# Three moves in the gated stage of a graph transformer: GpSimd's long third parts behind weight sums, and parts of the output weights behind gates and eviction sums

## The chip, the cores and the metric

The kernel runs on one core of a Trainium2 chip. The metric is the device time of one execution in microseconds (us). The core has a matrix engine (TensorE, PE in the profile), three engines for elementwise work (VectorE is DVE, ScalarE is ACT, GpSimd is POOL), and SyncE (SP), which here only issues transfers between the device's memory and the on-chip memory SBUF. Matmul results go to eight banks of another on-chip memory, PSUM. Each engine takes its own instructions strictly in order.

## The reference

A graph network with four transformer layers between two graph convolutions, on 1024 nodes with 512 features in float32. The change lies in the second half of each layer, the gated feed-forward part:

```python
for i in range(L):                                   # L = 4
    a = _attn(_ln(h, ln2_w[i], ln2_b[i]), cond, Wq[i], Wk[i], Wv[i], Wo[i])
    h = h + a
    u = _ln(h, ln3_w[i], ln3_b[i]) @ geglu_w[i] + geglu_b[i]   # 512 -> 4096
    val, gate = jnp.split(u, 2, axis=-1)
    f = val * jax.nn.gelu(gate, approximate=False)             # 2048 wide
    h = h + f @ ffo_w[i] + ffo_b[i]                            # 2048 -> 512
```

## The kernel before

**The gated stage.** For each layer, the product with `geglu_w` is cut into 4 x 4 pieces (r = 0 to 3, c = 0 to 3); each yields 128 columns of values and of gates on both halves of the nodes. The four pieces of r = 0 (class `Quad`) run first. The twelve of r = 1 to 3 are `Chunk` objects, named by layer, r and c; this text names one of layer 0 by r_c, so 3_3 is the last. A chunk is a fast scheme with seven products (numbers 0 to 6) in place of eight, and each float32 operand is split into three parts of a faster matmul form: a high part (`h`), a low part (`l`) and their difference (`s`, the third part). Each product is three pairs of matmuls: with h (first pair), with l (second), and, after ScalarE or VectorE has scaled the sum in its PSUM bank by 1 + TINY, with s. That makes 42 matmuls per chunk, 21 pairs. On the side of the nodes the parts (`gr`, `gl`) are there from the start. On the side of the weights each chunk's have to be made:

- SP loads the chunk's weights, `gxa` and `gxb` (`Chunk.__init__`, four transfers, called by `load()`).
- GpSimd forms the scheme's **sums** of the weights (`Chunk.sums`, L1097): three into `gxa`, one into `gy`, 128 x 256 each.
- ScalarE makes the high parts (L1060): `gha` (128 x 1024, the "long" one), `ghb` (128 x 512) and a 128 x 256 piece of `gs` from `gy` (the "short" ones).
- VectorE makes the low parts (L1061): `gla`, `glb`, and a piece of `gs`.
- GpSimd makes the third parts (L1066): `gsa` in two halves of 128 x 512, `gsb`, and a piece of `gs`.

A chunk uses gha, gla, gsa for products 0, 5, 6 and 4, ghb, glb, gsb for 1 and 3, gs for 2. All this is done ahead: while PE works at chunk m, the engines make the long parts of chunk m+1 and the sums of chunk m+2.

**Around the products.** `Chunk.steps` is a generator that the loop at the end of the listing drives step by step; the steps of chunk m-1 (`before` in the loop) are interleaved with those of chunk m (`flow`). ScalarE scales banks (L1139), copies product 0 (L1168) and applies the two gates, Gelu with a bias (L1152). VectorE adds products to running sums (L1160), does the scalings that take a term along, the **eviction sums** (L1143), and multiplies values by gates into the tile fT (L1191, L1193). SP stores fT to `f_dram` (L1209).

**The output stage** follows (class `Output`): eight units for each half of the nodes, each with a load `fr` of 256 columns of f and, in the first half, a load `wff` of 256 rows of `ffo_w`. Both are split in three: `ah_f` on ScalarE, `al_f`, `as_f` on VectorE for f (`Output.split`, L315 to L318); `bh_wff` on ScalarE, `bl_wff`, `bs_wff` on VectorE (two halves each) for the weights (`split_w`, L1244 to L1251). A unit is four blocks of six matmuls (L1270): bh with ah, bl with al, bs with as. Unit 0's weights are prepared during the gated stage: `ahead` yields after each of the five operations, one per chunk. f's first load is `output.fetch(0)`, its split `output.split(0)`; `fetch_w(u)` loads weights.

**What sets the order.** Instructions wrapped in `pin` stay in the order in which the program emits them, on their engine; the rest is placed by the scheduler at the times of its own model. So the order of the calls in the loop is by and large the order on each engine. `waiting_for(ins, engine)` makes all of GpSimd's instructions emitted in the block wait for `ins`: for the third parts that is `split_left.low`, the last low part made so far. The tiles come from a ring of 35 slots of 128 x 1024.

Of the kernel before, what the change touches and what calls it, by code (L numbers as in the profile page):

```python
# [26 lines left out]
def gnn_kernel(  # L27
# [37 lines left out]
    KC = D // P  # L65
# [4 lines left out]
    R = DFF // D  # L70
# [14 lines left out]
    @contextmanager  # L85
    def waiting_for(ins, engine):

        traced = nc.cur_bb.bb.instructions
        n = len(traced)
        yield  # L90
        for i in traced[n:]:
            if i.engine == engine:
                tc.add_manual_dep(i, ins.ins.name, mybir.DependencyInfo(
                    mybir.DependencyClass.Sync, mybir.DependencyReason.DATA))
# [454 lines left out]
    def project_steps(nb, hT, w, name, emit):  # L549

        ph = bank(f"hw_{name}_{nb}")
        c0 = (nb % 4) * P
        for k in range(KC):
            nc.tensor.matmul(ph, hT[nb // 4][k // 2][:, k % 2, c0:c0 + P],
                             w[k // 2][:, k % 2, :], start=(k == 0), stop=(k == KC - 1),
                             skip_group_check=True)
            yield
        emit(nb, ph)
# [132 lines left out]
    def add_left(left, rows, to, root, name):  # L691

        for d in range(NB):
            nc.sync.dma_start(left.rearrange("p a b -> p (a b)"), left_dram[d])
            pl = bank(f"left_{name}_{d}")
            for s in range(NB):
# [7 lines left out]
    steps = (step for nb in range(NB)  # L704
             for step in project_steps(nb, h0T, w_in, "in",
                                       lambda nb, ph: nc.scalar.copy(hs_in[nb], ph)))
# [11 lines left out]
    with ExitStack() as behind:  # L718
        for begun_by in (scaled_last, shifted_last):
            behind.enter_context(tc.issue_after(begun_by.ins))  # L720
        for t in range(ET):
            if t % (ET // (NB * KC)) == 0:
                next(steps)
            count(t)
        for _ in steps:
            pass
        first_v = bank("begun_v0")
        plain(first_v, raw_x[0, 0], 0, raw_wv, range(2))
        with tc.issue_after(load_dve.ins):
            for j in counted:  # L730
                if j % 2:
                    degrees(j // 2, C[j // 2], t512(f"part_{j // 2}"))
        with tc.issue_after(degrees.last.ins):
            plain(first_v, raw_x[0, 0], 0, raw_wv, range(2, KC))
        nc.scalar.copy(begun["v0"][0][:, 0, :], first_v)
# [66 lines left out]
    def acc_tile(name):  # L802
        return accs.tile([P, 512], F32, tag="acc", name=name)
# [271 lines left out]
    class Chunk:  # L1075
# [75 lines left out]
            cg = self.cv + DFF // P  # L1151
            pin(nc.scalar.activation(to, of, AF.Gelu, bias=gcols[:, cg:cg + 1]))  # L1152

        def steps(self, sum_next):


            n, bias = self.n, gcols[:, self.cv:self.cv + 1]

            def add(to, x, y):
                pin(nc.vector.tensor_tensor(to, x, y, OP.add))  # L1160

            self.banks = {}
            self.scale(0)
            yield
            self.scale(5)
            yield
            s1, u2, u3 = (acc_tile(f"g{x}_{n}") for x in ("s1", "u2", "u3"))
            pin(nc.scalar.copy(s1, self.end(0)))  # L1168
            self.scale(6)
            yield  # L1170
            add(u2, self.end(5), s1)
            yield
            sum_next()
            self.scale(4)
            add(u3, self.end(6), u2)
            self.scale_onto(1, s1)
            g1 = acc_tile(f"g1_{n}")
            d = self.end(4)
            add(g1, d, u3)
            add(u2, d, u2)  # L1180
            self.scale_onto(3, u3)
            self.scale_onto(2, u2)
            yield
            a = self.end(1)
            yield
            g0 = acc_tile(f"g0_{n}")
            self.gate(g0, self.end(3))
            self.gate(g1, g1)
            d = self.end(2)
            f0, f1 = self.f.of(self.c)  # L1190
            pin(nc.vector.scalar_tensor_tensor(f0, a, bias, g0, OP.add, OP.mult))  # L1191
            yield
            pin(nc.vector.scalar_tensor_tensor(f1, d, bias, g1, OP.add, OP.mult))  # L1193
            self.f.store(self.c)
# [263 lines left out]
    for l in range(L):  # L1458
# [261 lines left out]
        def load():  # L1720
            if chunks:
                ready.append(Chunk(l, *chunks.pop(0)))

        def sum_chunk(n):
            if n < len(ready):
                ready[n].sums()

        def begin_split(n, low, t=nc.gpsimd):
            flow = ready[n].split_steps(low, t) if n < len(ready) else iter(())
            next(flow, None)  # L1730
            return flow
# [7 lines left out]
        for c, q in enumerate(quads):  # L1739
            if c == 2:  # L1740
                long, short = (begin_split(0, low, nc.vector) for low in (False, True))
# [7 lines left out]
                load()  # L1749
        with waiting_for(split_left.last, mybir.EngineType.Pool):  # L1750
            sum_chunk(1)

        def split_rest(short):
            long = begin_split(0, False)
            next(long, None)
            with waiting_for(split_left.low, mybir.EngineType.Pool):
                for flow in short, long:
                    for _ in flow:
                        pass

        output = Output(l)
        ahead = output.ahead()
        before, short = None, iter(())
        for r in range(1, R):
            f = Gated(l, r)
            for c in range(KC):
                n = (r - R + 2) * KC + c
                if n == -1:
                    output.fetch_w(0)
                if (r, c) == (R - 1, KC - 2):  # L1770
                    output.fetch(0)
                chunk = ready.pop(0)
                flow = chunk.steps(lambda: sum_chunk(1))
                chunk.f = f
                next(flow)
                if 0 < n < 5:
                    next(ahead)
                for _ in islice(short, 2):
                    pass
                next(flow)  # L1780
                if before:
                    split_rest(short)
                    load()
                for _ in parts:
                    pass
                if (r, c) == (R - 1, KC - 1):
                    output.split(0)
                    output.fetch(1)
                for step in range(3):
                    if before:  # L1790
                        next(before, None)
                    next(flow)
                    if step == 0 and n == 0:
                        next(ahead)
                    if step == 1 and not before:
                        split_rest(iter(()))
                        load()
                before = flow
                short = begin_split(0, True)
        output.fetch_w(1)  # L1800
        output.fetch_w(2)
        for _ in range(3):
# [201 lines left out]
```

## Time and profile before

| what | value |
|---|---|
| median of 3 runs | 2320.28 us (2319.72 to 2321.01) |
| profiled execution's own time | 2319.71 us |
| its span, first to last instruction | 2317.9 us |
| granted TensorE clock, mean | 1.000 |
| gated chunks of layer 0 in the span | 445.49 to 565.76 us |
| PE busy in that window | 118.06 of 120.27 us |
| VectorE, ScalarE, GpSimd busy there | 108.47, 68.87, 89.52 us |

The profile is of one execution. A row of its timeline gives the start in us from the span's start, the duration, the engine, the line, the operation, and the tiles written and read, without their numbers; "x2" marks two merged instructions, and brackets say how long the engine was idle ahead of it and which instruction ended that. A row of the waits gives the total in us, the count and the longest. Matmul rows overlap: each is in the pipeline for longer than the interval to the next start, so starts are compared. One layer stands for all four: the stage begins at 445.49, 980.35, 1515.18 and 2049.99 us and takes 120.3 us each time.

### The profile page before, as it was taken

The page shows a single profiled execution, that of the slowest core. Times are in us where ns is not written, and L with a number is a line of the kernel's source. Part 1 is how long each engine was busy: PE and PEld are TensorE (multiplying, and loading weights), DVE is VectorE, ACT ScalarE, POOL GpSimd, SP SyncE. Part 2 cuts the span into 40 slices and gives each one's busy share as a digit, 9 for nine tenths or more (in the row PEclk, how much of TensorE's full clock was granted, in tenths as well). Part 3 has the DMA queues.
Part 4 walks back from the last instruction along what each step waited for, and adds up shares of the span by engine and source line. Part 5 has one row for each costly group of instructions (what it writes and reads, how often), then busy time and mean ns, then how long its engine had stood idle before and what let it go on. Part 6 is the DMA issues. An engine that isn't in the chain of part 4 may idle for free. (4 is left out here: it accounts for less than half of the span.)

```text
span 2317.9 us, 34192 instructions
## 1 busy us (share of the span) xinstructions
PE 2290.8 (99%) x12368; PEld 1730.7 (75%) x12368; DVE 1718.3 (74%) x3176; ACT 1101.5 (48%) x2159; POOL 799.7 (34%) x739
## 2 busy tenths in 40 slices
PE   8999999999999999999999999999999999999999
PEld 5668887577877887477886888577786888667777
DVE  9876556899975556989985555989986554889964
ACT  7544554565344445455344444556334444555410
POOL 1133223285032235177022334168022224158211
PEclk9999999999999999999999999999999999999999
DMA  6052120245411101134521111133532111033551
GB/s 204 2 160 87 55 96 6 69 119 177 151 64 65 54 24 37 56 117 128 182 82 69 53 40 37 35 107 106 182 135 69 36 43 51 10 109 119 182 191 37
DMA packets 161072, 205.46 MB, mean 89 GB/s; under 512 B 11304, under 2 KB 101744, under 8 KB 160896
## 3 DMA queue, kind: packets, MB, share of 16 engines
q1 hardware_dynamic: 158800, 197.77, 25.9%
q0 software_dynamic: 1376, 4.30, 0.6%
q8 instruction: 102, 1.67, 0.3%
q10 hardware_dynamic: 720, 1.11, 0.1%
q14 instruction: 74, 0.61, 0.1%
HBM read 152.80 MB, written 50.34 MB: 88 GB/s over the span
## 5 line engine op out<-in xcount | busy, mean ns | idle before, releaser
L321 POOL TENSOR_TENSOR as_c<-ah_c,al_c 128x512 fp32r<-128x512 f32 x128 | 191.5, 1526 | 405.1 <-DVE al_c L316 338.4
L1139 ACT ACTIVATE g<-g 128x512 f32<-128x512 f32 x192 | 112.5, 586 | 145.3 <-PE g L1125 145.3
L378 ACT ACTIVATE k<-k 128x512 f32<-128x512 f32 x125 | 72.2, 584 | 227.4 <-PE k L367 227.4
L1270 PE MATMUL fx<-bs_wff,as_f 128*128 128x512 f32 x512 | 158.9, 390 | 0.6 <-DVE as_f L318 0.6
L1270 PE MATMUL fy<-bl_wff,al_f 128*128 128x512 f32 x512 | 158.9, 390 | 0.6 <-DVE al_f L316 0.5
L1270 PE MATMUL fy<-bh_wff,ah_f 128*128 128x512 f32 x512 | 157.7, 389 | 0.2 <-ACT ah_f L315 0.2
L848 ACT ACTIVATE pr<-sc,nmax 128x256 f32<-128x256 f32 x256 | 118.4, 475 | 76.2 <-DVE nmax L843 75.5
L315 ACT ACTIVATE ah_f<-fr 128x1024 fp32r<-128x1024 f32 x64 | 67.9, 1060 | 176.2 <-PE fy L1270 101.0
L383 DVE COPY kT<-k 128x512 f32<-128x512 f32 x54 | 37.2, 688 | 143.9 <-PE k L367 143.9
L367 PE MATMUL v<-bh_wv,ah_c 128*128 128x512 f32 x508 | 142.8, 403 | 0.0
L367 PE MATMUL v<-bs_wv,as_c 128*128 128x512 f32 x508 | 142.2, 402 | 0.1
L367 PE MATMUL k<-ah_c,bh_wk 128*128 128x512 f32 x500 | 136.9, 395 | 0.0
L367 PE MATMUL v<-bl_wv,al_c 128*128 128x512 f32 x508 | 136.2, 390 | 0.0
L367 PE MATMUL k<-al_c,bl_wk 128*128 128x512 f32 x500 | 134.0, 390 | 0.0
L367 PE MATMUL k<-as_c,bs_wk 128*128 128x512 f32 x500 | 132.3, 395 | 0.2
L378 ACT ACTIVATE v<-v 128x512 f32<-128x512 f32 x127 | 75.0, 590 | 115.7 <-PE v L367 115.7
L853 DVE TENSOR_SCALAR pr<-pr,inv 128x256 f32<-128x256 f32 x256 | 127.3, 540 | 2.3
L1125 PE MATMUL g<-gr,gsa 128*128 128x512 f32 x384 | 122.8, 401 | 4.8 <-ACT g L1139 4.8
L1125 PE MATMUL g<-gr,gha 128*128 128x512 f32 x384 | 120.0, 394 | 0.0
L1125 PE MATMUL g<-gl,gla 128*128 128x512 f32 x384 | 118.4, 389 | 0.0
L1066 POOL TENSOR_TENSOR gsa<-gha,gla 128x512 fp32r<-128x512 f32 x88 | 112.4, 1300 | 16.9 <-DVE gla L1061 16.9
L920 POOL TENSOR_TENSOR os<-oT 128x256 f32<-128x256 f32 x12 | 8.8, 732 | 308.8 <-DVE oT L894 308.8
(360 smaller groups left out, 5828.6 us busy)
## 6 DMA issues: line engine op xcount, KB each, us to landing
f_dram<-fT SPq DMA_DIRECT2D x128, 256.0 KB, 2.6
fr<-f_dram SPq DMA_DIRECT2D x64, 512.0 KB, 4.2
ct<-cond_dram SPq DMA_DIRECT2D x48, 512.0 KB, 4.2
wff<-in_L_gnn_ffo_w_dram SPq DMA_DIRECT2D x32, 512.0 KB, 5.8
gxb<-in_L_gnn_geglu_w_dram SPq DMA_DIRECT2D x96, 128.0 KB, 2.6
gxa<-in_L_gnn_geglu_w_dram SPq DMA_DIRECT2D x96, 128.0 KB, 2.6
cond<-in_L_gnn_cond_dram SPq DMA_DIRECT2D x32, 256.0 KB, 4.5
cond_dram<-ct SPq DMA_DIRECT2D x16, 512.0 KB, 3.5
```

The lines of the kernel that those rows point to most:

```text
L315: nc.scalar.mul(twelve_bits(h), x, INWARD * TINY)
L321: nc.gpsimd.tensor_tensor(twelve_bits(s)[:, k, :], h[:, k, :], l[:, k, :], OP.subtract)
L367: pin(nc.tensor.matmul(self.bank, twelve_bits(left[k // 2])[:, k % 2, self.c * P:(self.c + 1) * P], twelve_bits(right[k // 2])[:, k % 2, : ...
L378: nc.scalar.mul(self.bank, self.bank, 1.0 + TINY)
L383: nc.vector.tensor_copy(self.to(), self.bank)
L848: nc.scalar.activation(pr3[:, a, :], ps3[:, a, :], AF.Exp, bias=nmax[:, a:a + 1], accum_out=tot[:, a:a + 1])
L853: scores.last = nc.vector.tensor_scalar(pr3[:, a, :], pr3[:, a, :], inv[:, a:a + 1], None, OP.mult)
L920: t.tensor_tensor(s1, a21, a22, OP.add)
L1066: split_left.last = pin(t.tensor_tensor(s_at, h_at, l_at, OP.subtract))
L1125: pin(nc.tensor.matmul(to, self.part(i, which)[:, k, :], self.rights[i][which].bitcast(F32R)[:, k, :], start=start and k == 0, stop=stop a ...
L1139: pin(nc.scalar.mul(to, to, 1.0 + TINY))
L1270: pin(nc.tensor.matmul(to, twelve_bits(left[which][0])[:, k, b * P:(b + 1) * P], twelve_bits(right[which])[:, k, :], start=u == 0 and whic ...
```

## The change

It has three parts, all in the loop over chunks:

1. In `split_rest` GpSimd does the sums of chunk m+2 after the short third parts of chunk m and ahead of the long third part (`gsa`) of chunk m+1; until now they came behind it, called from `Chunk.steps`. The load of a chunk moves along, ahead of the sums, and the third chunk's load moves ahead of the loop.
2. `next(ahead)` for the first operation on the output weights, `bh_wff_0` on ScalarE, moves from between a scaling and the gates to the end of the loop's turn.
3. `output.split(0)` (ah_f_0, al_f_0, as_f_0) and `output.fetch(1)` move from the middle of the last chunk's turn to its end.

The lines of the code after this point shift by one (L1209 becomes L1208). The diff:

```diff
--- before.py
+++ after.py
@@ -1151,7 +1151,7 @@
             cg = self.cv + DFF // P
             pin(nc.scalar.activation(to, of, AF.Gelu, bias=gcols[:, cg:cg + 1]))
 
-        def steps(self, sum_next):
+        def steps(self):
 
 
             n, bias = self.n, gcols[:, self.cv:self.cv + 1]
@@ -1170,7 +1170,6 @@
             yield
             add(u2, self.end(5), s1)
             yield
-            sum_next()
             self.scale(4)
             add(u3, self.end(6), u2)
             self.scale_onto(1, s1)
@@ -1749,14 +1748,19 @@
                 load()
         with waiting_for(split_left.last, mybir.EngineType.Pool):
             sum_chunk(1)
+        load()
 
         def split_rest(short):
             long = begin_split(0, False)
             next(long, None)
             with waiting_for(split_left.low, mybir.EngineType.Pool):
-                for flow in short, long:
-                    for _ in flow:
-                        pass
+                for _ in short:
+                    pass
+                if before:
+                    load()
+                sum_chunk(1)
+                for _ in long:
+                    pass
 
         output = Output(l)
         ahead = output.ahead()
@@ -1770,7 +1774,7 @@
                 if (r, c) == (R - 1, KC - 2):
                     output.fetch(0)
                 chunk = ready.pop(0)
-                flow = chunk.steps(lambda: sum_chunk(1))
+                flow = chunk.steps()
                 chunk.f = f
                 next(flow)
                 if 0 < n < 5:
@@ -1780,23 +1784,21 @@
                 next(flow)
                 if before:
                     split_rest(short)
-                    load()
                 for _ in parts:
                     pass
-                if (r, c) == (R - 1, KC - 1):
-                    output.split(0)
-                    output.fetch(1)
                 for step in range(3):
                     if before:
                         next(before, None)
                     next(flow)
-                    if step == 0 and n == 0:
-                        next(ahead)
                     if step == 1 and not before:
                         split_rest(iter(()))
-                        load()
                 before = flow
                 short = begin_split(0, True)
+                if n == 0:
+                    next(ahead)
+                if (r, c) == (R - 1, KC - 1):
+                    output.split(0)
+                    output.fetch(1)
         output.fetch_w(1)
         output.fetch_w(2)
         for _ in range(3):
```

GpSimd's order in the middle of the stage, around the long third part of chunk 2_3 (gsb and gs are those of 2_2; gxa and gy are the sums of 3_0):

```order
 L1066 TENSOR_TENSOR gsb_2_2_18980<-ghb_2_2_18978,glb_2_2_18979 128x512
 L1066 TENSOR_TENSOR gs_0_2_2_18977<-gs_0_2_2_18977 128x256
+L1097 TENSOR_TENSOR gxa_3_0_19005<-gxa_3_0_19005,gxb_3_0_19006 128x256
+L1097 TENSOR_TENSOR gxa_3_0_19005<-gxa_3_0_19005 128x256 x2
+L1097 TENSOR_TENSOR gy_3_0_19007<-gxb_3_0_19006,gxa_3_0_19005 128x256
 L1066 TENSOR_TENSOR gsa_2_3_19000<-gha_2_3_18998,gla_2_3_18999 128x512 x2
-L1097 TENSOR_TENSOR gxa_3_0_19007<-gxa_3_0_19007,gxb_3_0_19008 128x256
-L1097 TENSOR_TENSOR gxa_3_0_19007<-gxa_3_0_19007 128x256 x2
-L1097 TENSOR_TENSOR gy_3_0_19009<-gxb_3_0_19008,gxa_3_0_19007 128x256
```

The four sums now stand between gs and gsa. PE's order is the same in both kernels.

VectorE's order at the end of the stage, before; glb and gs are the last low parts, of chunk 3_3, and fT_3_2 is the product with the gates of the chunk before it:

```order
L1061 TENSOR_SCALAR glb_3_3_19478<-ghb_3_3_19477,gxb_3_3_19313 128x512
L1061 TENSOR_SCALAR gs_0_3_3_19476<-gs_0_3_3_19476,gy_3_3_19314 128x256
L316 TENSOR_SCALAR al_f_0_0_19499<-ah_f_0_0_19498,fr_0_19390 128x1024
L318 TENSOR_TENSOR as_f_0_0_19500<-ah_f_0_0_19498,al_f_0_0_19499 128x1024
L1191 TENSOR_SCALAR fT_3_2_19527<-g_0_3_2_19453,gcols,g_0_3_2_19520 128x512
L1160 TENSOR_TENSOR gu_0_3_3_19509<-g_0_3_3_19490,gs_0_3_3_19508 128x512
```

and after, from the last two eviction sums of chunk 3_3:

```order
L1143 TENSOR_SCALAR g_0_3_3_19547<-g_0_3_3_19547,gu_0_3_3_19502 128x512
L1143 TENSOR_SCALAR g_0_3_3_19553<-g_0_3_3_19553,gu_0_3_3_19501 128x512
L316 TENSOR_SCALAR al_f_0_0_19560<-ah_f_0_0_19559,fr_0_19390 128x1024
L318 TENSOR_TENSOR as_f_0_0_19561<-ah_f_0_0_19559,al_f_0_0_19560 128x1024
L1190 TENSOR_SCALAR fT_3_3_19580<-g_0_3_3_19536,gcols,g_0_3_3_19573 128x512
L1192 TENSOR_SCALAR fT_3_3_19580<-g_0_3_3_19553,gcols,g_0_3_3_19542 128x512
```

al_f and as_f of f's first load moved over a whole chunk of eviction work, from ahead of fT_3_2 to ahead of fT_3_3. On ScalarE ah_f_0 moved likewise, from ahead of the chunk's first scaling to behind the gates of chunk 3_2, ahead of the scaling of product 4.

SP's order there, before (each fT row is two stores; fr and wff are loads):

```order
L1228 DMA fr_0_19390<-f_dram 128x2x512
L1209 DMA f_dram<-fT_3_0_19340 256x1x256 x2
L1209 DMA f_dram<-fT_3_1_19436 256x1x256 x2
L1228 DMA fr_1_19504<-f_dram 128x2x512
L1238 DMA wff_1_19567<-in_L_gnn_ffo_w_dram 128x2x512
L1238 DMA wff_2_19569<-in_L_gnn_ffo_w_dram 128x2x512
L1209 DMA f_dram<-fT_3_2_19527 256x1x256 x2
L1228 DMA fr_2_19585<-f_dram 128x2x512
L1209 DMA f_dram<-fT_3_3_19580 256x1x256 x2
```

and after:

```order
L1227 DMA fr_0_19390<-f_dram 128x2x512
L1208 DMA f_dram<-fT_3_0_19344 256x1x256 x2
L1208 DMA f_dram<-fT_3_1_19436 256x1x256 x2
L1208 DMA f_dram<-fT_3_2_19519 256x1x256 x2
L1227 DMA fr_1_19565<-f_dram 128x2x512
L1237 DMA wff_1_19567<-in_L_gnn_ffo_w_dram 128x2x512
L1237 DMA wff_2_19569<-in_L_gnn_ffo_w_dram 128x2x512
L1208 DMA f_dram<-fT_3_3_19580 256x1x256 x2
L1227 DMA fr_2_19585<-f_dram 128x2x512
```

The loads fr_1, wff_1 and wff_2 now stand behind the stores of fT_3_2, and fr_2 behind those of fT_3_3.

## The prediction

> **What bounds the kernel now.** I read the page's busy shares first, then the waits, then the timelines of the stage that the change touches.
>
> ```profile
> span 2317.9 us, 34192 instructions
> PE 2290.8 (99%) x12368; PEld 1730.7 (75%) x12368; DVE 1718.3 (74%) x3176; ACT 1101.5 (48%) x2159; POOL 799.7 (34%) x739
> ```
> ```profile
> PE g L1125 <- ACT g L1139: 4.8, 8, 0.8
> PE g L1125 <- DVE g L1143: 4.0, 4, 1.0
> ```
>
> PE is the bound. Only time in which PE waits, or runs thinner than its matmuls allow, can be won or lost; the change leaves PE's own work and order alone. The visible waits of the chunked matmuls are 8.8 us over four layers, one long ACT wait and one long DVE wait in each.
>
> The larger part is spread thinly. The first and last row here are PE's first use of a long third part (gsa) in the second and in the last chunk of layer 0. I call that moment p.
>
> ```profile
> 456.41 0.62 PE L1125 MATMUL g<-gr,gsa 128*128 128x512 f32 x2
> ...
> 457.77 0.62 PE L1125 MATMUL g<-gr,gsb 128*128 128x512 f32 x2
> ...
> 555.29 0.61 PE L1125 MATMUL g<-gr,gsa 128*128 128x512 f32 x2
> ```
>
> From 456.41 to 457.77 lie three pairs of matmuls with nothing between them, so a pair takes 0.4533 us. A chunk has 21 pairs, 9.52 us; ten chunks need 95.2 us, and 98.88 us passed. So 3.7 us per layer lie in chunks longer than their matmuls; the other layers repeat this one. GpSimd and VectorE show why:
>
> ```profile
> 538.27 1.22 DVE L1061 SCALAR_TENSOR_TENSOR gla<-gha,gxa 128x1024 fp32r<-128x1024 f32 x1 [0.85 <-ACT gha L1060]
> ...
> 545.34 0.88 DVE L1061 SCALAR_TENSOR_TENSOR glb<-ghb,gxb 128x512 fp32r<-128x512 f32 x1
> ...
> 547.94 1.23 DVE L1061 SCALAR_TENSOR_TENSOR gla<-gha,gxa 128x1024 fp32r<-128x1024 f32 x1 [0.84 <-ACT gha L1060]
> ```
> ```profile
> 539.64 1.31 POOL L1066 TENSOR_TENSOR gsb<-ghb,glb 128x512 fp32r<-128x512 f32 x1 [1.61 <-PE g L1125]
> ...
> 541.60 2.56 POOL L1066 TENSOR_TENSOR gsa<-gha,gla 128x512 fp32r<-128x512 f32 x2
> 544.10 0.76 POOL L1097 TENSOR_TENSOR gxa<-gxa,gxb 128x256 f32<-128x256 f32 x1
> 544.93 1.88 POOL L1097 TENSOR_TENSOR gxa<-gxa 128x256 f32<-128x256 f32 x2
> ```
>
> GpSimd waits for gla, makes gsb, gs, the two halves of gsa, then the sums; ScalarE's gha waits for those sums, and gla waits for gha. One turn of that ring is 547.94 - 538.27 = 9.67 us, 0.15 over PE's 9.52. I call the start of gla G.
>
> **The new order of the ring.** With sums ahead of gsa, gha has its sums early and the ring through ScalarE no longer binds. In its place stands VectorE's own order, and gsa comes later. The prices:
>
> ```profile
> 445.61 0.74 POOL L1097 TENSOR_TENSOR gxa<-gxa,gxb 128x256 f32<-128x256 f32 x1 [15.13 <-DVE gs L1066]
> ...
> 447.95 0.74 POOL L1097 TENSOR_TENSOR gy<-gxb,gxa 128x256 f32<-128x256 f32 x1
> ...
> 556.17 2.15 POOL L1066 TENSOR_TENSOR gsb<-ghb,glb 128x512 fp32r<-128x512 f32 x1 [2.35 <-DVE gs L1061]
> ```
> ```profile
> 497.15 1.23 DVE L1061 SCALAR_TENSOR_TENSOR glb<-ghb,gxb 128x512 fp32r<-128x512 f32 x1
> ...
> 555.01 0.68 DVE L1061 SCALAR_TENSOR_TENSOR glb<-ghb,gxb 128x512 fp32r<-128x512 f32 x1
> ```
>
> Undisturbed, the sums take 447.95 - 445.61 + 0.74 = 3.08 us. A glb of VectorE takes 0.68 us where GpSimd is idle (555.01) and 1.23 where GpSimd makes sums (497.15); a gsb of GpSimd takes 1.31, and 2.15 beside al_f. So VectorE's operations on SBUF and GpSimd's exclude each other and take turns: the one that waits ends about 0.55 us (VectorE) or 0.85 to 1.15 us (GpSimd, 512 wide) after the other. gsa beside VectorE's reads of PSUM is not stretched (541.60: two halves in 2.56).
>
> From G: GpSimd starts its third operation at +3.33 (541.60 - 538.27), so sums until +6.37, first half of gsa until +7.67, call it G+7.70 at PE. glb asks at +6.84 to +7.07 (545.34), falls into that first half, and ends at +8.2; the second half ends at +9.35, gs at +9.6, and gla follows at G+9.55. That is a turn of 9.55 in place of 9.67, with the second half ready 1.1 us before its matmuls need it (six pairs, 2.72 us, after p).
>
> In four chunks of a layer VectorE also has a part of the output weights (bl_wff or bs_wff) ahead of glb. Then it gives way twice: part until +8.2, second half until +9.35, glb +9.9, gs, gla at G+10.16. So p can only follow G by 7.70, with turns of 9.55 (six) and 10.16 (four). Its start: gla of the second chunk at 451.57 leaves G alone, and gsa, now behind 3.08 us of sums, moves that chunk's p from 456.41 to about 457.3, a loss of 0.9.
>
> ```profile
> 489.39 1.04 ACT L1244 ACTIVATE bh_wff<-wff 128x1024 fp32r<-128x1024 f32 x1
> ...
> 491.04 0.75 DVE L1191 SCALAR_TENSOR_TENSOR fT<-g,gcols,g 128x512 f32<-128x512 f32 x1 [1.28 <-ACT g L1152]
> ```
>
> Moving bh_wff_0 behind the gates takes away the 1.04 us by which it delays the gates (VectorE's 1.28 idle at 491.04); behind ghb it lies in ScalarE's idle time, so it costs nothing until VectorE's part of the next chunk, 4 us later. I count it as won inside the turns above.
>
> Together: the loss of 0.9 and 4 x (10.16 - 9.52) = 2.6 and six times 0.03 give an excess of 3.6 where 3.7 is now. I work p of the last chunk out as 555.21 against 555.29: the ring comes out even, -0.1 us per layer. Bounds: if glb follows the part at once and the turn is 9.55 throughout, -2.5; if a turn with a part becomes 10.55 (rival B), +2.6 with the start.
>
> **The end of the stage.**
>
> ```profile
> 557.37 1.30 ACT L1152 ACTIVATE g<-g,gcols 128x512 f32<-128x512 f32 x2
> ...
> 565.15 1.30 ACT L1152 ACTIVATE g<-g,gcols 128x512 f32<-128x512 f32 x2 [5.43 <-PE g L1125]
> ```
> ```profile
> 555.95 1.22 DVE L316 SCALAR_TENSOR_TENSOR al_f<-ah_f,fr 128x1024 fp32r<-128x1024 f32 x1
> ...
> 559.33 0.74 DVE L1191 SCALAR_TENSOR_TENSOR fT<-g,gcols,g 128x512 f32<-128x512 f32 x1
> ...
> 563.63 1.28 DVE L1143 SCALAR_TENSOR_TENSOR g<-g,gu 128x512 f32<-128x512 f32 x2
> ...
> 567.43 1.23 DVE L316 SCALAR_TENSOR_TENSOR al_f<-ah_f,fr 128x1024 fp32r<-128x1024 f32 x1
> 568.69 1.23 DVE L318 TENSOR_TENSOR as_f<-ah_f,al_f 128x1024 fp32r<-128x1024 f32 x1
> ...
> 572.49 1.22 DVE L316 SCALAR_TENSOR_TENSOR al_f<-ah_f,fr 128x1024 fp32r<-128x1024 f32 x1
> ...
> 577.00 0.69 DVE L1251 SCALAR_TENSOR_TENSOR bs_wff<-bh_wff,bl_wff 128x512 fp32r<-128x512 f32 x1
> ```
>
> With al_f_0 and as_f_0 gone from 555.95, VectorE's next work, fT of chunk 3_2, waits for the first of its two gates (557.37 + 0.65) and starts at 558.0 instead of 559.33. Its chain to the last eviction sum is 564.91 - 559.33 = 5.58 us, so that ends at 563.58, and PE leaves the last chunk 1.5 us earlier. But the same two operations, 1.23 us each, now stand there: as_f_0 is ready at 566.08, where PE would want it at about 565.0, two pairs after the chunk's end. fT_3_3 starts at 566.0, al_f_1 at 567.3 (567.43 now). VectorE is the bound from here through unit 1, and its work has hardly become less, so of the 1.5 us only about 0.13 survives. ah_f_0, moved in front of a scaling on ScalarE, delays that by 0.4 us; PE's need of it is just met.
>
> The transfers pay. SP issues in order:
>
> ```profile
> 561.35 1.19 SPq L1209 DMA_DIRECT2D f_dram<-fT  x2
> 562.59 0.61 SPq L1228 DMA_DIRECT2D fr<-f_dram  x1
> 567.31 1.18 SPq L1209 DMA_DIRECT2D f_dram<-fT  x2
> 568.53 0.62 SPq L1238 DMA_DIRECT2D wff<-in_L_gnn_ffo_w_dram  x1
> ```
> ```profile
> fr<-f_dram SPq DMA_DIRECT2D x64, 512.0 KB, 4.2
> wff<-in_L_gnn_ffo_w_dram SPq DMA_DIRECT2D x32, 512.0 KB, 5.8
> ```
> ```profile
> DMA to landing us min/median/max: 3.9/5.7/8.3
> ```
>
> The first two lines are the medians of the page, issue to landing; the last is of the six fr loads between 550 and 580 us, a time in which many loads run together.
>
> fr_1, wff_1 and wff_2 move behind the stores of fT_3_2: fr_1 is issued at about 561.25 and lands at 565.5, wff_1, issued at 561.85, at 567.65, both about when ScalarE comes to them (the gates at 565.15 come 1.5 us earlier, with ah_f_1 behind them; bh_wff_1 is wanted by VectorE at 569.7). fr_2 moves behind the stores of fT_3_3, which wait for VectorE: those go out at 567.4, fr_2 1.24 us later (562.59 - 561.35), at 568.65, six microseconds after its present 562.59. With 4.2 us it lands at 572.85, ah_f_2 (1.06) ends at 573.95, al_f_2 starts at 574.0 instead of 572.49. bs_wff_2, four operations on, ends at 579.2 instead of 577.69; PE wants it then:
>
> ```profile
> 577.53 0.62 PE L1270 MATMUL fy<-bl_wff,al_f 128*128 128x512 f32 x2
> 577.98 0.62 PE L1270 MATMUL fx<-bs_wff,as_f 128*128 128x512 f32 x2
> 578.43 0.61 PE L1270 MATMUL fy<-bh_wff,ah_f 128*128 128x512 f32 x2
> ```
>
> The second block of unit 2, 578.43 now, starts at about 579.6: +1.15 us per layer, which already holds the -0.1 of the ring and the -0.13 of the end. I take 4.2, the median over all layers, since only two stores stand just ahead, as ahead of the fr_2 of now, which is the 3.9. Landing after 3.9 us would make it +0.85; after 5.7, the median in the burst, +2.65. fr_3 and the later loads have slack: they are issued 1.4 us later, and al_f_4 is not wanted for another 4 us. By the Trainium skill, "DMA: Bandwidth & Descriptors", section "Anatomy of one DMA", a transfer costs 2.0 us plus its bytes at 436 GB/s; as an estimate that is 3.2 us here, and the loss per layer would be about 0.2 instead of 1.15, 1 us in all. The trace's 4.2 (median) disagrees, and decides.
>
> Sum: 4 x 1.15 = +4.6 on the profiled execution's 2319.7, so 2324.3. The median of the runs, 2320.28, is 0.6 above that execution: **2325**.
>
> **The rivals.**
>
> A, faster: VectorE keeps its turn. If part and glb pass one after the other and only then the second half of gsa, the turn with a part is about 9.55, gsa's second half at +9.96 still comes in time (p + 2.72 = +10.4). Then p of the last chunk is 457.3 + 95.5 = 552.8, 2.5 us earlier; less the 1.15 + 0.1 of fr_2, -1.25 per layer, 2315. It decides the case if, in chunks with a part, gla follows gla by under 9.8. Against it: 496.55 to 498.64 in the trace, where each side waited for one operation of the other, not two.
>
> B, slower: GpSimd comes half a microsecond later to gsa (sums of loads still landing, or a gsb that waits for PE, as at 539.64). Then part or glb goes first at +6.84, the first half of gsa ends at +8.66, and the chunk with a part turns in 10.55: one loss of 1.0 and four of 0.4, +2.6 and the +1.15, 3.75 per layer, 2335. The margin is 6.84 - 6.37 = 0.47 us. The Trainium skill, "SBUF — State Buffer", section "Who interferes with whom", says that whichever issues first gets the shared pair for its whole instruction; by it too this margin decides, and the stretched rows above agree.
>
> C, the transfers hide: fr_2 lands early enough (under 2.8 us, or VectorE's chain in front is faster than I have it), and the ring is even. Then nothing moves but -0.2 per layer: 2319.5 by the runs' median. Against it stands the shortest fr of that window, 3.9.
>
> **Chances.** Forecast (2322 to 2329) 0.42, A (2312 to 2318) 0.23, B (2331 to 2338) 0.22, C 0.13. About 0.2%, 4.6 us, is what a measurement of this kernel tells from no change; the forecast sits on that edge, so half of it counts as same: same 0.21 + 0.13 + 0.03 of A, slower 0.21 + 0.22, faster 0.2. The range 2314 to 2336 leaves out the outer parts of A and B.
>
> **What would show it.** gha without a wait for GpSimd; PE's first gsa matmul of each chunk waiting for GpSimd, 7.7 us behind gla; turns of 9.55 and 10.16; the bh_wff wait gone; the wait for an eviction sum replaced by one for as_f_0; fr_2 issued near 568.6 and PE waiting in unit 2 for bl_wff and bs_wff. Wrong: PE waits for gsa by over 1 us per chunk, or unit 2 has no gap.

## The result and the profile after

| | before | after |
|---|---|---|
| median of the runs, us | 2319.68 (10 runs) | 2326.52 (10 runs) |
| ratio, 95% interval | | 1.003 (1.002 to 1.0039) |
| profiled execution's own time, us | 2319.71 | 2326.6 |
| its span, us | 2317.9 | 2324.8 |
| first matmul of the gated stage, layers 0 to 3 | 445.49, 980.35, 1515.18, 2049.99 | 445.58, 982.72, 1518.77, 2055.42 |

The changed kernel is slower by 6.8 us; 4.7 were forecast. From one stage's first matmul to the next a layer takes 2.28, 1.22 and 1.84 us more than before, and the rest behind the last start takes 1.4 more. The kernels below are compared by these distances, since the work ahead of the first stage varies by some 0.8 us between executions of most of them.

The page after, its line of busy shares, and four of PE's rows of its waits:

```profile
PE 2291.8 (99%) x12368; PEld 1730.7 (74%) x12368; DVE 1751.6 (75%) x3176; ACT 1105.5 (48%) x2159; POOL 784.6 (34%) x739
```
```profile
PE g L1125 <- POOL gsa L1066: 6.2, 18, 0.7
...
PE fy L1269 <- DVE bl_wff L1246: 3.8, 6, 0.8
...
PE fx L1269 <- DVE as_f L318: 2.7, 5, 0.6
...
PE k L367 <- ACT k L378: 0.8, 1, 0.8
```

Both of the waits shown before (4.8 for ScalarE's scaling, 4.0 for an eviction sum) are gone. In their place PE waits for gsa 18 times, for the output weights' low parts and for as_f. The first of these rows looks like the whole loss, 6.2 against 6.8. The experiments show that it isn't.

PE in layer 0: the first gsa matmul of the second and of the last chunk, the start of the output stage, and unit 2.

```profile
457.30 0.73 PE L1125 MATMUL g<-gr,gsa 128*128 128x512 f32 x2 [0.64 <-POOL gsa L1066]
...
555.28 0.62 PE L1125 MATMUL g<-gr,gsa 128*128 128x512 f32 x2
...
564.37 0.62 PE L1269 MATMUL fy<-bh_wff,ah_f 128*128 128x512 f32 x2
...
566.12 0.73 PE L1269 MATMUL fx<-bs_wff,as_f 128*128 128x512 f32 x2 [0.53 <-DVE as_f L318]
566.69 0.62 PE L1269 MATMUL fy<-bh_wff,ah_f 128*128 128x512 f32 x2
...
579.01 0.50 PE L1269 MATMUL fy<-bl_wff,al_f 128*128 128x512 f32 x1 [0.82 <-DVE bl_wff L1246]
...
580.07 0.62 PE L1269 MATMUL fy<-bh_wff,ah_f 128*128 128x512 f32 x2
```

VectorE in one turn with a part of the output weights, in the last turn, and at the stage's end:

```profile
518.18 1.21 DVE L1061 SCALAR_TENSOR_TENSOR gla<-gha,gxa 128x1024 fp32r<-128x1024 f32 x1
...
524.83 1.55 DVE L1250 SCALAR_TENSOR_TENSOR bs_wff<-bh_wff,bl_wff 128x512 fp32r<-128x512 f32 x1
...
526.30 1.77 DVE L1061 SCALAR_TENSOR_TENSOR glb<-ghb,gxb 128x512 fp32r<-128x512 f32 x1
...
528.33 1.22 DVE L1061 SCALAR_TENSOR_TENSOR gla<-gha,gxa 128x1024 fp32r<-128x1024 f32 x1
...
537.87 1.21 DVE L1061 SCALAR_TENSOR_TENSOR gla<-gha,gxa 128x1024 fp32r<-128x1024 f32 x1
...
544.51 1.54 DVE L1061 SCALAR_TENSOR_TENSOR glb<-ghb,gxb 128x512 fp32r<-128x512 f32 x1
...
547.41 1.21 DVE L1061 SCALAR_TENSOR_TENSOR gla<-gha,gxa 128x1024 fp32r<-128x1024 f32 x1
...
563.59 1.22 DVE L316 SCALAR_TENSOR_TENSOR al_f<-ah_f,fr 128x1024 fp32r<-128x1024 f32 x1
...
565.98 0.74 DVE L1190 SCALAR_TENSOR_TENSOR fT<-g,gcols,g 128x512 f32<-128x512 f32 x1
...
574.54 1.23 DVE L316 SCALAR_TENSOR_TENSOR al_f<-ah_f,fr 128x1024 fp32r<-128x1024 f32 x1 [2.10 <-ACT ah_f L315]
```

GpSimd in that last turn, its last sum and then the two halves of gsa:

```profile
543.52 0.74 POOL L1097 TENSOR_TENSOR gy<-gxb,gxa 128x256 f32<-128x256 f32 x1
544.22 2.99 POOL L1066 TENSOR_TENSOR gsa<-gha,gla 128x512 fp32r<-128x512 f32 x2
```

And SyncE, with the landing time of the fr load issued there from the view of that tile:

```profile
567.41 1.18 SPq L1208 DMA_DIRECT2D f_dram<-fT  x2
568.72 0.54 SPq L1227 DMA_DIRECT2D fr<-f_dram  x1
```
```profile
DMA to landing us min/median/max: 4.6/4.6/4.6
```

The ring of weights turns as worked out: 9.54 us without a part (537.87 to 547.41) and 10.15 with one (518.18 to 528.33). The last eviction sums are done 1.3 us earlier than before (al_f follows them at 563.59; before they ended at 564.91), PE waits 0.53 us for as_f, fr_2 goes out at 568.72 instead of 562.59, VectorE sits 2.10 us idle for it, and unit 2's second block starts at 580.07 instead of 578.43. Counted from the stage's start, the whole course of layer 0 is this: unit 0 begins 1.32 us earlier than before (118.79 against 120.11), its second block only 0.36 us earlier (121.11 against 121.47), unit 2 still 0.26 us earlier, and unit 2's second block 1.54 us later (134.49 against 132.95; 1.25, 1.76 and 1.33 in the other layers). So the wait for as_f costs PE 0.96 us, though the view shows 0.53, and unit 2's first block, where the data of fr_2 comes late, costs it 1.80.

### The profile page after: what moved, and what is told of

The parts are those of the page before. It is cut to its first block, busy times and chain, and to the rows that moved or that the text cites. A ratio compares the mean times of both kernels' runs of the same rounds, so it can differ in the third digit from the quotient of the medians.

```text
span 2324.8 us, 34205 instructions
## 1 busy us (share of the span) xinstructions
PE 2291.8 (99%) x12368; PEld 1730.7 (74%) x12368; DVE 1751.6 (75%) x3176; ACT 1105.5 (48%) x2159; POOL 784.6 (34%) x739
## 5 line engine op out<-in xcount | busy, mean ns | idle before, releaser
L1066 POOL TENSOR_TENSOR gsa<-gha,gla 128x512 fp32r<-128x512 f32 x88 | 129.8, 1497 | 0.0
L1269 PEld LDWEIGHTS fy<-bl_wff,al_f 128*128 128x128 f32 x512 | 95.7, 188 | 30.0 <-DVE bl_wff L1246 8.6
```

The source lines that it names most:

```text
L1066: split_left.last = pin(t.tensor_tensor(s_at, h_at, l_at, OP.subtract))
L1269: pin(nc.tensor.matmul(to, twelve_bits(left[which][0])[:, k, b * P:(b + 1) * P], twelve_bits(right[which])[:, k, :], start=u == 0 and whic ...
```

## The experiments

Two theories stood at first. T: the loss comes from part 3 (output split and fetch at the end of the turn), through the late fr_2 and as_f; the ring is about even. G: the loss is what the waits name, GpSimd's gsa behind the sums (part 1). The runs below are ordered by what they tell apart. "Per layer" compares the distances of the stage starts with those of before.

| kernel | median us | kernel before beside it | ratio (95%) | per layer, us |
|---|---|---|---|---|
| part 1 alone | 2316.27 | 2318.93 | 0.9990 (0.9981 to 0.9999) | -0.62, -0.81, -0.68 |
| parts 1 and 2 | 2315.73 | 2318.93 | 0.9987 (0.9978 to 0.9996) | -1.05, -0.95, -0.85 |
| part 3 alone | 2325.82 | 2318.93 | 1.0029 (1.0017 to 1.0040) | +1.55, +1.40, +1.29 |
| changed, split(0) put back | 2315.41 | 2319.18 | 0.9984 (0.9975 to 0.9993) | -1.16, -0.87, -0.96 |
| changed, fr_2 early | 2320.66 | 2318.93 | 1.0016 (0.9999 to 1.0033) | -0.05, -0.19, +0.82 |
| changed, fr_2 one place later | 2336.67 | 2319.18 | 1.0072 (1.0059 to 1.0086) | +4.08, +4.25, +4.71 |
| parts 1 and 2, sums between gsa's halves | 2305.14 | 2319.18 | 0.9942 (0.9928 to 0.9955) | -3.40, -3.53, -3.50 |
| part 1 alone, sums between gsa's halves | 2307.15 | 2320.17 | 0.9947 (0.9933 to 0.9961) | -3.19, -3.26, -3.05 |
| parts 1 and 2, sums between gsa's halves, fr_0 a chunk earlier | 2306.64 | 2320.17 | 0.9944 (0.9931 to 0.9958) | -3.09, -3.08, -3.09 |

### Part 3 undone: parts 1 and 2 alone

```diff
--- after.py
+++ parts 1 and 2
                 for _ in parts:
                     pass
+                if (r, c) == (R - 1, KC - 1):
+                    output.split(0)
+                    output.fetch(1)
                 for step in range(3):
...
                 if n == 0:
                     next(ahead)
-                if (r, c) == (R - 1, KC - 1):
-                    output.split(0)
-                    output.fetch(1)
```

> The changed kernel with its third part undone: output.split(0) and output.fetch(1) are back in the middle of the last chunk's turn, GpSimd's new order and the new place of bh_wff_0 stay. Theory T (transfer): the loss is the load fr_2, which stands behind the stores of the last chunk; with it back ahead of them the loss is gone, and the new ring alone is even: 2319.3, within 1 us of before. Rival G (GpSimd): the waits of PE for gsa, 6.2 us in the waits of the changed kernel, are the loss; they stay, so 2325 to 2326.

Measured: 2315.73, 0.9987 of before. G is out: PE's waits for gsa are all still there, and the kernel is faster than before. Two of PE's rows of its waits:

```profile
PE g L1125 <- POOL gsa L1066: 6.5, 19, 0.7
PE g L1125 <- DVE g L1143: 1.2, 4, 0.3
```

T is right on the place and off on the size: the ring doesn't come out even, it gains about 0.95 us per layer. In layer 0 the last chunk's first gsa matmul comes 109.65 us after the stage's start (before 109.80), so up to there it is indeed even. The gain comes behind it. The wait for an eviction sum, 1.0 us in each layer before, is 0.3 here, because VectorE comes earlier to the last sums. Its last gla starts 101.79 us behind the stage's start, and 102.45 before. From the last gsa use to unit 0 it takes 9.43 us (554.49 to 563.92) and took 10.31 (555.29 to 565.60). PE there, in this kernel and then in the one before:

```profile
554.49 0.61 PE L1125 MATMUL g<-gr,gsa 128*128 128x512 f32 x2
...
562.69 0.73 PE L1125 MATMUL g<-gr,gsb 128*128 128x512 f32 x2 [0.29 <-DVE g L1143]
...
563.92 0.62 PE L1269 MATMUL fy<-bh_wff,ah_f 128*128 128x512 f32 x2
```
```profile
564.38 0.74 PE L1125 MATMUL g<-gr,gsb 128*128 128x512 f32 x2 [1.00 <-DVE g L1143]
...
565.60 0.62 PE L1270 MATMUL fy<-bh_wff,ah_f 128*128 128x512 f32 x2
```

### Part 1 alone

```diff
--- after.py
+++ part 1 alone: part 3 undone as above, and
                     next(flow)
+                    if step == 0 and n == 0:
+                        next(ahead)
                     if step == 1 and not before:
...
                 short = begin_split(0, True)
-                if n == 0:
-                    next(ahead)
```

> The changed kernel with its second and third parts undone, so GpSimd's new order alone; bh_wff_0 stands ahead of the gates again. T: the ring is now VectorE's own turn, so the 1 us by which bh_wff_0 delays the gates goes into one turn per layer in full (a turn of about 11.1 in place of 10.16): +0.6 to +1 us per layer, 2322 to 2323.5. G: 2325 or more. If the new order gained by itself, it would be under 2319.

Measured: 2316.27, 0.5 us over the kernel with part 2. The price set for bh_wff_0 in its old place was too high. The turn that holds it takes 10.30 us there and 10.16 behind the gates, and ScalarE's long wait of PE (4.8 us in all before) is gone in both: it went with the sums' new place, not with bh_wff_0's.

### Part 3 alone

```diff
--- before.py
+++ part 3 alone
                 for _ in parts:
                     pass
-                if (r, c) == (R - 1, KC - 1):
-                    output.split(0)
-                    output.fetch(1)
                 for step in range(3):
...
                 short = begin_split(0, True)
+                if (r, c) == (R - 1, KC - 1):
+                    output.split(0)
+                    output.fetch(1)
```

> The kernel before with the third part of the change alone: output.split(0) and output.fetch(1) at the end of the last chunk's turn. T: fr_2 is as late as in the changed kernel, so all of the loss is here, about 1.7 us per layer: 2326 to 2327. G: no wait for gsa comes in, so 2319 to 2320.

Measured: 2325.82, 1.0029. Part 3 by itself costs what the whole change costs. PE's waits of this kernel (its lines are numbered as in the kernel before):

```profile
PE g L1125 <- ACT g L1139: 4.8, 8, 0.8
PE fy L1270 <- DVE bl_wff L1247: 3.3, 4, 0.8
```

The row for eviction sums is missing here as it is after the change. So parts 1 and 2 and part 3 cure the same wait: part 3 by taking al_f_0 and as_f_0 from ahead of the sums, parts 1 and 2 by bringing VectorE there earlier. Together they cure it once. The start of unit 0 shows it, counted from the stage's start in layer 0: 120.11 us before, 119.08 with parts 1 and 2, 118.78 with part 3 alone, and 118.79 with all three, so beside part 3 the other two win nothing there. That is why a gain of 3.2 us and a loss of 6.9 add up to a loss of 6.8 and not of 3.7.

### Which of part 3's two calls

```diff
--- after.py
+++ changed, split(0) put back
                 for _ in parts:
                     pass
+                if (r, c) == (R - 1, KC - 1):
+                    output.split(0)
                 for step in range(3):
...
                 if (r, c) == (R - 1, KC - 1):
-                    output.split(0)
                     output.fetch(1)
```

> The changed kernel with output.split(0) back in the middle of the last chunk's turn and output.fetch(1) alone at its end. fr_2 then stands ahead of the last chunk's stores, wff_2 behind those of the chunk before. V: what costs in the third part is the split on VectorE and ScalarE, in its own place and through fr_2, not the fetch: as without the third part, 2315 to 2317. Rival F: the fetch is what makes fr_1, wff_1, wff_2 and fr_2 late: 2320 or more.

Measured: 2315.41, as without part 3. `output.fetch(1)` at the end of the turn costs nothing; `output.split(0)` costs all of it. The scheduler's order says the same the other way round: with split(0) at the turn's end fr_2 stands behind the stores of fT_3_3 even when fetch(1) is back in its old place (a kernel that was not run). So it is moving the split's operations that moves fr_2, a load which the scheduler places by the times of its own model.

### fr_2 by itself: early, and later still

The first of these keeps the change and issues fr_2 ahead of the last chunk's remaining steps, so ahead of the stores of fT_3_3:

```diff
--- after.py
+++ changed, fr_2 early
         output.fetch_w(1)
         output.fetch_w(2)
+        output.fetch(2)
         for _ in range(3):
             next(before, None)
...
             for n in range(2 * UNITS):
-                output.fetch(n + 2)
+                if n:
+                    output.fetch(n + 2)
```

> The changed kernel with one transfer moved: fr_2 is issued ahead of the stores of the last chunk, all else as changed. T: fr_2 goes out at about 563 instead of 568.7, the gaps of PE in unit 2 go, and what is left is -0.1 (ring) and -0.15 (end) per layer: 2318.5 to 2319.5. G: the waits for gsa are still there: 2325 to 2326.5.

Measured: 2320.66, 1.7 us over the kernel before beside it, where the changed kernel was 6.8 over. One of its eleven runs took 2341.93 us, at a mean clock of 0.948, and widens the interval. SyncE and PE at the end of layer 0's gated stage:

```profile
562.52 0.42 SPq L1227 DMA_DIRECT2D fr<-f_dram  x1
...
566.83 1.18 SPq L1208 DMA_DIRECT2D f_dram<-fT  x2
```
```profile
563.78 0.61 PE L1269 MATMUL fy<-bh_wff,ah_f 128*128 128x512 f32 x2
...
565.54 0.73 PE L1269 MATMUL fx<-bs_wff,as_f 128*128 128x512 f32 x2 [0.52 <-DVE as_f L318]
566.10 0.62 PE L1269 MATMUL fy<-bh_wff,ah_f 128*128 128x512 f32 x2
```

fr_2 is where it was, and the waits of unit 2 are gone. One of 0.8 us is left in unit 1 of the third layer, where the load fr_1 takes 5.6 us to land (4.1 to 4.7 in the others). The wait for as_f stays in each layer. The view names 0.5 us for it, but unit 0's first block takes 2.32 us (563.78 to 566.10) where it takes 1.36 with parts 1 and 2 alone. That is 0.96 us; the unit begins 0.3 us earlier, so about 0.7 is left of the 0.8 to 1.7 us per layer that separate the two kernels, and the third layer has the wait for fr_1 on top.

The second moves fr_2 one place back, behind the third load of output weights:

```diff
--- after.py
+++ changed, fr_2 one place later
             for n in range(2 * UNITS):
-                output.fetch(n + 2)
+                if n:
+                    output.fetch(n + 2)
                 output.split(n + 1)
                 output.fetch_w(n + 3)
+                if not n:
+                    output.fetch(n + 2)
```

> The changed kernel with fr_2 one place later still, behind the load wff_3: issued 0.6 us later and with 512 KB more in front of it. T: PE waits in unit 2 for as long as fr_2 is late, so +0.6 to +1.4 us per layer: 2329 to 2332. Rival: the gap in unit 2 is VectorE's own work, whatever the load does: 2326.5.

Measured: 2336.67, 10.2 us over the changed kernel, a good deal more than the load's delay and outside both forecasts. One row of PE's waits, then PE's matmuls in unit 2, and the windows there (columns: window, its length, busy us and count of PE, PEld, DVE, ACT and POOL, granted TensorE clock, DMA share, GB/s):

```profile
PE fy L1269 <- DVE bl_wff L1246: 8.7, 9, 1.5
```
```profile
581.14 0.49 PE L1269 MATMUL fy<-bl_wff,al_f 128*128 128x512 f32 x1 [1.05 <-DVE bl_wff L1246]
...
582.47 0.55 PE L1269 MATMUL fy<-bl_wff,al_f 128*128 128x512 f32 x1 [0.83 <-DVE bl_wff L1246]
582.81 1.18 PE L1269 MATMUL fx<-bs_wff,as_f 128*128 128x512 f32 x2
...
586.28 0.62 PE L1269 MATMUL fy<-bh_wff,ah_f 128*128 128x512 f32 x2
```
```profile
579.00:582.80 3.80, 1.92 (x7) 1.05 (x6) 3.70 (x6) 3.34 (x4) 0.00 (x0) 1.00 1.05 391
582.80:584.00 1.20, 1.20 (x4) 0.71 (x3) 1.20 (x2) 0.49 (x2) 0.00 (x0) 0.50 1.04 384
584.00:586.40 2.40, 2.40 (x7) 1.88 (x7) 2.33 (x4) 1.00 (x1) 0.00 (x0) 0.54 0.99 317
```

al_f_2 starts 0.96 us later than in the changed kernel, counted from the stage's start. The rest is the clock: behind the longer wait four pairs take 3.47 us (582.81 to 586.28) where 4 x 0.4533 = 1.81 would do, so 1.66 us. Together that is 2.6 per layer, and four times that is 10.4, near the 10.2 measured. The other layers show the same: the clock is 0.50 from 1122.1 to 1125.5, 1661.4 to 1664.8 and 2200.7 to 2204.1 us, and unit 2's third block comes 2.34, 3.01, 2.57 and 2.85 us later than in the changed kernel, each counted from its stage's start.

### The long third part cut in half

G was wrong on the sign, but not on everything. Where each chunk's turn takes 9.55 or 10.15 us and 21 pairs need 9.52, the wait for gsa is PE's remaining loss. Its first half is all that PE needs at p. Two views stood: G, that the half ahead of the sums frees the turns, and V, that VectorE then bounds them and hardly anything is won. The edit, on parts 1 and 2 alone:

```diff
--- parts 1 and 2
+++ sums between gsa's halves
                 for _ in short:
                     pass
+                next(long, None)
                 if before:
                     load()
                 sum_chunk(1)
                 for _ in long:
                     pass
```

> The changed kernel with its third part undone and GpSimd's sums between the two halves of gsa: first half, sums, second half. Theory V: VectorE's own turn (9.55 us, 10.15 with a part of the output weights) is now the bound of the stage and the waits of PE for gsa only show it; PE's waits for gsa (6.5 us in the kernel without the third part) should go, but the time only falls by what the collisions on VectorE shrink and by what the first chunk's 0.9 us is worth at the end: 2313 to 2315.7. Rival G: the waits for gsa are themselves the cost, so 6.5 us go with them: about 2309.

Measured: 2305.14, 0.9942 (0.9928 to 0.9955), faster than both kernels and below both forecasts; G came nearer. GpSimd and VectorE in one turn, then PE at the first gsa use of the second and of the last chunk and at the one wait that is left in the chunks:

```profile
538.20 1.29 POOL L1066 TENSOR_TENSOR gsa<-gha,gla 128x512 fp32r<-128x512 f32 x1
...
541.77 1.07 POOL L1097 TENSOR_TENSOR gy<-gxb,gxa 128x256 f32<-128x256 f32 x1
542.81 1.47 POOL L1066 TENSOR_TENSOR gsa<-gha,gla 128x512 fp32r<-128x512 f32 x1
```
```profile
533.79 2.31 DVE L1061 SCALAR_TENSOR_TENSOR gla<-gha,gxa 128x1024 fp32r<-128x1024 f32 x1
...
543.14 2.23 DVE L1061 SCALAR_TENSOR_TENSOR gla<-gha,gxa 128x1024 fp32r<-128x1024 f32 x1
```
```profile
455.72 0.62 PE L1125 MATMUL g<-gr,gsa 128*128 128x512 f32 x2
...
551.38 0.62 PE L1125 MATMUL g<-gr,gsa 128*128 128x512 f32 x2
...
560.15 0.74 PE L1125 MATMUL g<-gr,gsb 128*128 128x512 f32 x2 [0.87 <-DVE g L1143]
```

Ten chunks take 95.66 us, 9.57 each, where they took 98.88 before and 97.98 after the change. The first half is ready about 2 us ahead of its use (538.20 + 1.29, and PE comes to it at about 541.8, one chunk of 9.57 before 551.38; 2.0 to 3.4 us over the layer's chunks). Behind a first turn of 6.22 the ring still turns unevenly, by 8.17 to 10.27, but with these 2 us in hand PE doesn't follow it. Those nine turns of VectorE average 9.56 ((543.14 - 457.10) / 9), PE's own pace, so VectorE does not bound the stage there; V was wrong on that. Against parts 1 and 2 the kernel is 10.6 us faster, more than the 6.5 us of waits for gsa that the view named there. PE comes to the last gsa use 3.07 us per layer earlier (106.58 us behind the stage's start, 109.65 there), and 0.6 of that goes back into the wait for the last eviction sums (0.87 here, 0.29 there). So the view named about half of what the late gsa cost. gla takes 2.31 us now in place of 1.21, since it starts beside GpSimd's second half of gsa. These 1.1 us are about what a half takes (1.29 to 1.47), as if gla waited for it on the way; they cost nothing.

The same order without part 2, that is with bh_wff_0 in its old place:

```diff
--- part 1 alone
+++ part 1 alone, sums between gsa's halves
                 for _ in short:
                     pass
+                next(long, None)
                 if before:
                     load()
```

> The kernel before with GpSimd's order first half of gsa, sums, second half, and nothing else of the change (bh_wff_0 ahead of the gates, split and fetch in their old places). If the gain of the 2305 us kernel is the place of the first half, ready 3 us before PE wants it, it is nearly all here: 2305 to 2307. If the new place of bh_wff_0 carries a part, 2307 to 2310.

Measured: 2307.15, 13.0 us under the kernel before beside it; the kernel with part 2 is 14.0 under its own. Nearly all of the gain is the order on GpSimd; the place of bh_wff_0 is worth 1 to 2 us at most, and the intervals of the two kernels overlap.

The wait that is left, 3.4 us in all, is for the last eviction sums. The last try loads and splits f's first piece a chunk earlier:

```diff
--- sums between gsa's halves
+++ fr_0 a chunk earlier
-                if (r, c) == (R - 1, KC - 2):
+                if (r, c) == (R - 1, KC - 3):
                     output.fetch(0)
...
-                if (r, c) == (R - 1, KC - 1):
+                if (r, c) == (R - 1, KC - 2):
                     output.split(0)
+                if (r, c) == (R - 1, KC - 1):
                     output.fetch(1)
```

> The kernel with the sums between the halves of gsa (2305 us), and output.fetch(0) and output.split(0) one chunk earlier, so that al_f_0 and as_f_0 stand behind the last gla. PE still waits 0.9 us per layer for the last eviction sums there. If VectorE has those 2.4 us to spare one turn earlier, that wait goes and up to 1.1 us per layer with it: 2301 to 2303. If it has not, the wait only moves into the chunk before, or grows: 2305 to 2309.

Measured: 2306.64, no gain. The wait for eviction sums falls from 3.4 to 1.8, and the chunk in which al_f_0 and as_f_0 now stand takes 10.73 us instead of 9.57: VectorE has no room for them there either.

## Why the prediction was right, and where it was not

**The ring.** Each number held: p at 457.30 (457.3 worked out) and at 555.28 (555.21), turns of 9.54 and 10.15 (9.55 and 10.16). In the turn with a part, bs_wff gives way to the first half of gsa until 518.18 + 8.20, glb to the second until +9.89, and gla follows at +10.15, as the double giving way had it. Rival A, turns under 9.8, did not come. Rival B did not either, though the margin was thin: GpSimd started the last turn's gsa at 544.22 and VectorE's glb at 544.51, 0.3 us apart where 0.47 was worked out.

**"The ring comes out even", as the worth of part 1.** This was wrong, by about 0.7 us per layer for part 1 alone and 0.95 with part 2. I measured the ring where gsa ties PE to gla, at p of the last chunk, and there it is even. What parts 1 and 2 win lies 9 us later, in the wait for an eviction sum. In the changed kernel this error doesn't show, because part 3 had already removed that wait. That the total came out near without the parts priced singly is luck in this respect: without part 3 the same sum would have missed the gain.

**bh_wff_0.** I put ScalarE's wait down to it. It goes without part 2 as well, and the new place saves 0.14 us in one turn.

**The end of the stage.** The rows fell within 0.1 us of those worked out: al_f_0 at 563.59 (563.58), fT_3_3 at 565.98 (566.0), and PE waiting for as_f_0. PE leaves the last chunk 1.3 us earlier, not 1.5 (the prediction's own rows give 564.91 - 563.58 = 1.33). That little of it survives was right: 0.36 us at unit 0's second block, 0.26 at unit 2, where the ring's 0.1 and the end's 0.13 had been counted.

**fr_2.** The mechanism and the issue time (568.72; 568.65 worked out) were right, and putting the load back takes away 5.1 of the 6.8 us (each against the kernel before beside it). The mis-sized term is the +1.15 per layer. I took a landing of 4.2 us; the four layers show 4.64, 4.00, 4.04 and 4.42, 4.28 on average. Counted from the stage's start the load lands on average 0.33 us later than worked out, and 0.25 of that is its issue: in the second and third layer the two stores ahead of it take SyncE 1.57 and 1.99 us instead of 1.18. From its landing to unit 2's second block it is 6.7 us in every layer, as worked out (579.6 - 572.85 = 6.75). So that block comes 1.47 us later than before on average ((1.54 + 1.25 + 1.76 + 1.33) / 4), 0.32 over the 1.15, and the later landing is all of it. Of the first layer's 2.28, 0.7 is another thing: a wait of PE for ScalarE's `k` (the row of 0.8) in the next layer's attention, which the sum didn't have and no run explains. Four times 0.32 and this 0.7 are nearly the 2.1 us by which the forecast fell short. Rival C, that the transfer hides, needed a landing under 2.8 us and met none under 4.0. By the Trainium skill, "DMA: Bandwidth & Descriptors", section "Anatomy of one DMA", whose fit is for transfers on the GpSimd path, the load would land in 3.2 us, an estimate from its fixed 2.0 us and its rate; these loads, which SyncE issues, took 0.8 to 1.4 us more.

## What to carry to other kernels

A producer whose consumer needs only its first half at once is cut there, with other work between the halves: in this kernel that order, on one engine, gave 13 to 14 us against the kernel before, where whole sums ahead of the whole producer gave 3. Price each part of a change with the others absent, since two parts can cure the same wait and then count once; and a wait that the view names may be as long in a faster kernel, or cost twice what the view says. When elementwise work is moved, look at which stores end behind it and which loads are queued behind those stores.

## What the hardware showed beside this

PE's clock fell to half behind waits that are short one by one. In the kernel with fr_2 one place later no gap of PE reaches 1.5 us, yet from 579.00 to 582.80 it was busy for only 1.92 of 3.80 us, and the clock granted next was 0.50 to 0.54 for 3.5 us. In the changed kernel's unit 2 the clock stayed full:

```profile
577.00:580.00 3.00, 2.02 (x7) 0.85 (x6) 2.93 (x6) 2.28 (x4) 0.00 (x0) 1.00 1.05 391
```

Part 3 alone met it once, in layer 3, where the rest behind the last stage start took 2.9 us more than before:

```profile
2236.00:2239.00 3.00, 1.63 (x6) 0.70 (x5) 2.45 (x2) 0.26 (x1) 0.00 (x0) 1.00 1.11 403
2239.00:2243.00 4.00, 4.00 (x11) 3.13 (x12) 2.39 (x2) 1.06 (x1) 0.00 (x0) 0.57 0.97 350
```

The same place in the kernel before (2230.90 to 2233.90, busy 1.86 of 3.00) kept the full clock. By the Trainium skill, "TensorE: Matmul & The Clock Gate", section "Part 1: The HAM clock gate", the clock is set by activity in free-running windows of about 3.4 us and halves after an idle one; the traces agree on the half clock and on the windows: in each of the eleven traces all changes of the clock lie whole multiples of 3.413 us apart. But no idle window was needed here. Cut into those windows, and with the tail of each execution left aside, the traces show the clock halved behind all five full-clock windows in which PE was busy for 0.33 to 0.45 of the time (all in the kernel with fr_2 one place later, one of them ahead of the first stage), and behind none of the seven with 0.47 to 0.56. The window behind which part 3 alone was halved had 0.60, so the busy share of the profile doesn't decide it alone, and why it fell there stays open.
